# The early rows gathered into the root products' tile, and the pool of row buffers opened inside the branch

## The chip, the cores and the metric

The kernel runs on one core of one Trainium2 chip. The metric is the device time of one execution in microseconds; where several executions are compared, their median is used.

## What is computed

A graph of 6250 nodes with 256 features each and 100000 edges, sorted by their destination. Three layers of message passing, then a layer norm over the sum with the input. Cut to what matters:

```python
ew = edge_attr @ edge_w + edge_b                      # 100000 x 256, from 32 attributes
rel_masks = [(edge_type == i) for i in range(3)]
inv_cnt = [1.0 / max(segment_sum(m, dst), 1.0) for m in rel_masks]
for l in range(3):
    residual = x
    msg = relu(x[src] * ew)
    out = 0
    for i in range(3):
        h = segment_sum(msg * rel_masks[i][:, None], dst) * inv_cnt[i][:, None]
        out = out + h @ weights[l, i]
    out = out + x @ roots[l] + biases[l]
    x = residual + relu(out)
return layernorm(x_in + x)
```

## The kernel before

**Units of work.** The edges are cut into tiles of 128; two tiles are a *pair* (391 pairs), and two pairs share one buffer of gathered rows, a tile named `xs` of 128 x 2 x 2 x 256 floats, 4 KB in each partition. Nodes are cut into 49 tiles of 128. `schedule` (L879) writes out by hand in which order the pairs are taken (`order`: pairs 64 to 390, then 63 down to 0; below, "pair n" is the n-th in this order) and at which step each node tile is finished (`starts`).

**Ahead of the branch.** `tile_gnn_resnorm_kernel` (L934) loads the indices, brings them into the layout of the tiles (`src_i`, `seg`, `place_i`), and tests whether the edges are sorted closely enough (`flag`). The branch at L1072 then runs `ordered_path`; `general_path` is for other inputs and doesn't run here. While the test is still under way, the rows of the first six pairs (`FIRST`, L873) are gathered already (L1017 to L1021): `room` (L921) asks the pool `rows` for a buffer, `gather_pair` (L926) issues two indirect DMAs from GpSimd's queue, one for each tile of 128 edges. Six pairs make twelve gathers and three buffers. The pool has `ROWS` = 8 buffers and is opened at L966, ahead of the branch.

**Inside the branch** one loop per layer (L784) walks over the pairs, one pair a step, and issues for several pairs at once, each at its own distance ahead:

- 9 pairs ahead (`AHEAD`, L463), `gather` (L589): for a layer's first six pairs it takes the buffers that were filled early, else, at every second pair, a new buffer by `room`, and the two gathers of L928. GpSimd has hardly any other work, so its queue holds these gathers one after the other; a gather into a buffer waits for the last reader of the buffer's earlier content.
- 7 and 6 pairs ahead, in layer 0 alone: the edge attributes are transposed on TensorE (L607) and kept by ScalarE (L615), and written to DRAM for the other layers.
- 4 pairs ahead, `make_ew` (L617): TensorE forms the edge weights in PSUM (L623).
- 3 pairs ahead, `weigh` (L641, VectorE, L645) multiplies the gathered rows in place by the edge weights, and `bound` (L647, ScalarE, L649) applies the relu in place.
- 2 pairs ahead, `one_hot` (L651): VectorE makes the matrices of destinations.
- `reduce` (L661): TensorE sums the rows of the pair by destination and relation into PSUM (L665); it is the last reader of the buffer. In layer 0 it also counts the edges (the bf16 products).
- one or two pairs behind (`LAG`), `add` (L670): VectorE adds the sums into the ring `acc` (L683).

**Root products and node tiles.** For each node tile, x @ roots + bias is formed ahead of time (`root_turn`, `root_turned`, `root_mul`, `root_keep`, L685 to L699) and kept in one of the `ROOTS` = 24 places of `x_root` (L487), 1 KB each in a partition. The place is `at_root` (L775). When a node tile's edges are all summed, `node_mul` and `node_end` (L703, L734) multiply by the weights, add to the place in `x_root` (L742), apply the relu and the residual (L745) and write the tile to `x_mid` in DRAM (L747), from where the next layer gathers.

**From layer to layer.** The first six pairs of the next layer are gathered at the end of a layer (`gather_early`, L627), into buffers of the same pool, before node tile 0 is done; what node tile 0 lacks is added afterwards (`complete`, L633). All other gathers of the next layer wait until `x_mid` is written to the end.

The order of the instructions on each engine is as the program issues them; buffers and waits between engines are set by the tile framework.

Of the kernel before, what the change touches and what calls it, by code (L numbers as in the profile page):

```python
# [8 lines left out]
F32 = mybir.dt.float32  # L9
# [430 lines left out]


@with_exitstack
def ordered_path(ctx, tc, x, edge_attr, weights, roots, biases, edge_w, edge_b, out, src, src_i, seg, place_i, consts, rows,
                 first_rows, node_i):


# [4 lines left out]
    P = 128  # L451
    N, D = x.shape
# [20 lines left out]
    ident, ones, iota_w = consts  # L473
# [6 lines left out]
    big = ctx.enter_context(tc.tile_pool(name="big", bufs=1))  # L480
# [3 lines left out]
        nc.scalar.dma_start(ew_sb[row + A:row + A1, :], edge_b[None, :])  # L484

    x_all = big.tile([P, NT, D], F32, name="x_all")
    x_root = big.tile([P, ROOTS, D], F32, name="x_root")  # L487


    acc = big.tile([P, DC + 1, R, ASIDE + 2 * P + WIN], F32, name="acc")  # L490
# [23 lines left out]
    came_i = came.bitcast(I32)  # L514

    edge = ctx.enter_context(tc.tile_pool(name="edge", bufs=2))
    wpool = ctx.enter_context(tc.tile_pool(name="wpool", bufs=1))
    o_pool = ctx.enter_context(tc.tile_pool(name="o_p", bufs=1, space=PSUM))
    r_pool = ctx.enter_context(tc.tile_pool(name="r_p", bufs=1, space=PSUM))
# [53 lines left out]
    def layer(l, r_sb, b_sb, ats, early, pools):  # L573
# [198 lines left out]

        node_at = {s: c for c, s in enumerate(starts)}
        turns_of = [node_at[s] for s in sorted(node_at)]
        at_root = {c: j % ROOTS for j, c in enumerate(turns_of)}  # L775
        root_at = {}

        for j, c in enumerate(turns_of):
# [78 lines left out]
    with tc.manual_schedule():  # L857
        state = (*load_root(0), {}, first_rows)
        for l in range(L):
            with ExitStack() as pools:  # L860
                state = layer(l, *state, pools)
# [8 lines left out]
ROOTS = 24  # L870
GROUP = 8
ROWS = 8
FIRST = 6  # L873
# [5 lines left out]
def schedule(N, E, lag):  # L879

    P = 128
    U = -(-E // (2 * P))
    NT = -(-N // P)
    done = []
    for c in range(NT):
        edges = E * min(1.0, (P * (c + 1) / N) ** 0.5)  # L890
        done.append(U if c == NT - 1 else min(U, -(-int(edges) // (2 * P)) + 4))
    K = -(-done[0] // GROUP) * GROUP
    order = list(range(K, U)) + list(range(K - 1, -1, -1))
    moved = done[1] - K + lag
    starts = [0] * NT
    step = moved
    for c in range(2, NT):
        step = starts[c] = max(done[c] - K + lag + 1, step + 4)

    whole = U - int(0.55 * K)  # L900
    starts[1] = max(whole + lag, step + 4)
    starts[0] = max(U + lag - 1, starts[1] + 4)

    node = lambda e: int(N * min(1.0, max(0.0, e / E)) ** 2)
    least = [node(2 * P * u - ASTRAY) for u in range(U)]
    most = [node(2 * P * u + ASTRAY) for u in range(U)]


    for p, u in enumerate(order, lag):
        if u >= K:  # L910
            assert all(p <= starts[c] or least[u] >= P * (c + 1) for c in range(2, NT))
            assert p <= moved or least[u] >= 2 * P
            assert all(p < starts[c] or least[u] >= P * c for c in range(8, NT, 8))
            for b in range(RING // P + 1, (most[u] + WIN - 1) // P + 1):
                assert (moved + 2 if b - RING // P == 1 else starts[b - RING // P] + 3) < p
        else:
            assert most[u] <= 2 * P and (p <= starts[1] or most[u] + WIN <= P)
    return order, starts, moved, least, most


def room(rows, D):  # L921

    return rows.tile([128, 2, 2, D], F32, name="xs", bufs=ROWS)


def gather_pair(nc, xs, x_rows, src_i, u):  # L926
    for i in range(2):
        nc.gpsimd.indirect_dma_start(  # L928
            out=xs[:, u % 2, i, :], out_offset=None, in_=x_rows[:, :],
            in_offset=bass.IndirectOffsetOnAxis(ap=src_i[:, 2 * u + i:2 * u + i + 1], axis=0))  # L930
# [3 lines left out]
def kernel(ctx, tc, x, src, dst, edge_attr, edge_type, weights, roots, biases, edge_w,  # L934
# [4 lines left out]
    P = 128  # L939
    N, D = x.shape  # L940
# [11 lines left out]
    keep = ctx.enter_context(tc.tile_pool(name="keep", bufs=1))  # L952
    ident = keep.tile([P, P], F32, name="ident_o")
    make_identity(nc, ident)
    ones = keep.tile([1, P], F32, name="ones_o")
    nc.vector.memset(ones, 1.0)
    iota_w = keep.tile([P, WK], F32, name="iota_w")
    nc.gpsimd.iota(iota_w, pattern=[[1, WK]], base=0, channel_multiplier=0,
                   allow_small_or_imprecise_dtypes=True)
    node_i = keep.tile([P, 1], F32, name="node_i")  # L960
    nc.gpsimd.iota(node_i, pattern=[[0, 1]], base=0, channel_multiplier=1, allow_small_or_imprecise_dtypes=True)
    src_i = keep.tile([P, TC], I32, name="src_io")
    seg = keep.tile([P, TC], F32, name="seg_o")
    place_i = keep.tile([1, (U + 1) // 2], I32, name="place_i")
    flag = keep.tile([1, 1], I32, name="flag")
    rows = ctx.enter_context(tc.tile_pool(name="rows", bufs=ROWS))  # L966

    with tc.tile_pool(name="look", bufs=1) as look, tc.tile_pool(name="look_p", bufs=2, space=PSUM) as look_p, \
            tc.manual_schedule():
# [47 lines left out]
        first_rows = {}  # L1017
        for u in schedule(N, E, 1)[0][:FIRST]:
            if u // 2 not in first_rows:
                first_rows[u // 2] = room(rows, D)  # L1020
            gather_pair(nc, first_rows[u // 2], x, src_i, u)  # L1021
        dst_t = by_tile("dst")

# [47 lines left out]
    unordered = nc.values_load(flag[0:1, 0:1], min_val=0, max_val=1)  # L1071
    with tc.If(unordered == 0):  # L1072
        ordered_path(tc, x, edge_attr, weights, roots, biases, edge_w, edge_b, out, src, src_i, seg, place_i,
                     (ident, ones, iota_w), rows, first_rows, node_i)
    with tc.If(unordered > 0):
        general_path(tc, x, src, dst, edge_attr, edge_type, weights, roots, biases, edge_w, edge_b, out)

# [25 lines left out]
```

## Time and profile before

| | us |
|---|---|
| median of 3 runs | 3021.46 (3019.87 to 3021.53) |
| the profiled execution | 3018.21 |
| its span, first to last instruction | 3016.4 |
| mean granted TensorE clock | 0.942 |

| engine | busy us | share of the span |
|---|---|---|
| TensorE, matmuls (PE) | 2789.6 | 92% |
| TensorE, weight loads (PEld) | 2252.3 | 75% |
| VectorE (DVE) | 2080.6 | 69% |
| ScalarE (ACT) | 987.1 | 33% |
| GpSimd (POOL) | 2236.2 | 74% |

The costliest groups of instructions are these; each row has the line, the engine and the operation, what is written and read, the count, and after the bar the busy time, the mean time of one in ns, and the engine's idle time ahead of them.

```profile
L928 POOL DMA_INDIRECT xs<-x_mid,src_io x1564 | 1488.9, 952 | 503.5 <-issue 416.8
...
L665 PE MATMUL h_p<-oh,xs 128*128 128x120 f32 x9384 | 1346.3, 295 | 28.2 <-DVE acc L683 12.5
...
L645 DVE TENSOR_TENSOR xs<-ew_p,xs 128x512 f32<-128x512 f32 x1176 | 753.2, 682 | 558.1 <-DMA xs<-x_mid,src_io 362.0
...
L928 POOL DMA_INDIRECT xs<-in_x_dram,src_io x782 | 745.5, 953 | 255.3 <-issue 198.9
```

Times in the profile are microseconds from the start of the span. In a timeline each row gives the start, the duration, the engine, the line, the operation, what it writes and reads, and in brackets how long the engine sat idle before it and what ended that. "issue" stands for idle time that the profile puts down to nothing. In the views of the waits a row gives the engine, what waited, what for, the total in us, the number of times and the longest. A table by stage gives for each stretch its length, the busy time of PE, PEld, DVE, ACT and POOL with the number of instructions, the granted TensorE clock, the DMA engines' share and the GB/s moved. Layer 0 runs to about 1003 us, layer 1 to about 2003, layer 2 to the end.

### The profile page before, as it was taken

Reading aid. Unit: us, or ns where it says so; the run is one execution under the profiler, and the core shown is the slowest. Engines: PE = TensorE matmul, PEld = TensorE weight load, DVE = VectorE, ACT = ScalarE, POOL = GpSimd, SP = SyncE. Lnnn points to the kernel's source line nnn. Section 1 sums busy time; section 2 is a strip of 40 time slices with the busy share of each in tenths; the row PEclk is TensorE's granted clock in tenths of the full one; section 3 lists DMA queues with packets and bytes.
Section 4 is the critical chain, followed back from the end, with each engine's and each line's share of the span. In section 5 each row is a group of like instructions: output and inputs, shape, how many; then the busy total and the mean of one; then the engine's idle time right before and its main releaser. Section 6 shows DMA issues by size and latency. Waiting matters only on the chain.

```text
span 3016.4 us, 55782 instructions
## 1 busy us (share of the span) xinstructions
PE 2789.6 (92%) x18114; PEld 2252.3 (75%) x18114; DVE 2080.6 (69%) x5865; ACT 987.1 (33%) x1354; POOL 2236.2 (74%) x2355
## 2 busy tenths in 40 slices
PE   6899999999999889999999999889999999999997
PEld 5777878888877667777777777667777777777775
DVE  6676767777776556666666667556667777877765
ACT  4444444444444222222222222212222222322221
POOL 6777777777777677777777777767777777777775
PEclk9999999999999899999999999878999999999888
DMA  5655555555555444444444445434554444444443
GB/s 154 176 162 161 166 165 151 149 158 156 159 156 145 144 125 137 139 132 140 134 142 144 144 137 149 151 116 140 151 149 146 147 147 149 142 144 144 135 139 97
DMA packets 274682, 438.87 MB, mean 145 GB/s; under 512 B 145004, under 2 KB 180032, under 8 KB 274384
## 3 DMA queue, kind: packets, MB, share of 16 engines
q0 software_dynamic: 112608, 307.65, 35.1%
q1 hardware_dynamic: 154720, 119.64, 13.4%
q10 hardware_dynamic: 7056, 7.92, 0.9%
q8 instruction: 149, 2.44, 0.3%
q14 instruction: 149, 1.22, 0.1%
HBM read 389.94 MB, written 45.09 MB: 144 GB/s over the span
## 4 chain that ended last, share of the span: by engine, by line
PE 56%; DMA 16%; POOL 10%; issue 8%; DVE 7%; ACT 2%; DVEq 0%; ACTq 0%; POOLq 0%; SPq 0%
PE h_p L665 25%; PE ew_p L623 16%; DMA xs<-x_mid,src_io 12%; POOL xs L928 10%; PE o_p L711 9%; DVE xs L645 4%; DMA xs<-in_x_dram,src_io 4%; PE r_p L696 3%; PE turn_p L607 1%; ACT xs L649 1%; DVE x_root L742 1%; DVE acc L683 1%; PE r_p L688 1%; PE o_p L637 0%; PE o_p L715 0%
## 5 line engine op out<-in xcount | busy, mean ns | idle before, releaser
L928 POOL DMA_INDIRECT xs<-x_mid,src_io x1564 | 1488.9, 952 | 503.5 <-issue 416.8
L665 PEld LDWEIGHTS h_p<-oh,xs 128*128 128x128 f32 x9384 | 1214.2, 204 | 245.9 <-issue 190.0
L665 PE MATMUL h_p<-oh,xs 128*128 128x120 f32 x9384 | 1346.3, 295 | 28.2 <-DVE acc L683 12.5
L649 ACT ACTIVATE xs<-xs 128x1024 f32<-128x1024 f32 x588 | 620.2, 1055 | 1857.3 <-DVE xs L645 1792.3
L645 DVE TENSOR_TENSOR xs<-ew_p,xs 128x512 f32<-128x512 f32 x1176 | 753.2, 682 | 558.1 <-DMA xs<-x_mid,src_io 362.0
L623 PE MATMUL ew_p<-ew_sb,at 33*128 33x256 f32 x4692 | 861.0, 418 | 151.3 <-DVE xs L645 149.2
L928 POOL DMA_INDIRECT xs<-in_x_dram,src_io x782 | 745.5, 953 | 255.3 <-issue 198.9
L623 PEld LDWEIGHTS ew_p<-ew_sb,at 33*128 33x128 f32 x4692 | 502.5, 191 | 393.8 <-DVE xs L645 192.1
L683 DVE TENSOR_TENSOR acc<-h_p,acc 128x240 f32 (+1 forms) x1173 | 517.7, 441 | 209.7 <-PE h_p L665 125.3
L655 DVE TENSOR_SCALAR oh<-iota_w,seg_o 128x120 f32<-128x120 f32 x2346 | 512.9, 293 | 0.0
L711 PE MATMUL o_p<-w_sb,acc 128*128 128x256 f32 (+1 forms) x1716 | 442.4, 395 | 4.9 <-DVE acc L683 4.9
L711 PEld LDWEIGHTS o_p<-w_sb,acc 128*128 128x128 f32 (+1 forms) x1716 | 319.1, 198 | 41.7 <-DVE acc L683 6.3
L742 DVE SCALAR_TENSOR_TENSOR x_root<-o_p,inv,x_root 128x256 f32<-128x256 f32 (+1 forms) x429 | 205.7, 480 | 47.0 <-PE o_p L711 39.4
L696 PE MATMUL r_p<-r_sb,t_s 128*128 128x256 f32 x588 | 160.7, 397 | 0.1
L659 ACT ACTIVATE oh_b<-oh 128x480 bf16<-128x480 f32 x196 | 117.9, 602 | 101.3 <-DVE oh L655 99.6
L728 ACT ACTIVATE acc<-zero_o 128x768 f32<-128x768 f32 (+1 forms) x150 | 140.5, 937 | 29.1 <-PE r_p L711 19.1
L696 PEld LDWEIGHTS r_p<-r_sb,t_s 128*128 128x128 f32 x588 | 106.6, 202 | 9.2 <-ACT t_s L692 0.3
L665 PE MATMUL h_p<-oh_b,full_ones 128*128 128x120 bf16 x782 | 107.5, 220 | 0.0
L607 PE MATMUL turn_p<-ident_o,an 128*128 128x128 f32 x391 | 79.4, 286 | 10.7 <-DMA an<-in_edge_attr_dram 6.1
L665 PEld LDWEIGHTS <-full_ones 128*128 128x128 bf16 x782 | 81.9, 105 | 2.5
L699 DVE TENSOR_TENSOR x_root<-r_p,b_sb 128x256 f32<-128x256 f32 x147 | 61.1, 416 | 24.0 <-PE r_p L696 19.5
L615 ACT ACTIVATE at<-turn_p 128x256 f32<-128x256 f32 x196 | 71.7, 366 | 2.7 <-PE turn_p L607 2.7
(93 smaller groups left out, 526.6 us busy)
## 6 DMA issues: line engine op xcount, KB each, us to landing
at<-at_all SPq DMA_DIRECT2D x96, 512.0 KB
xs<-x_mid,src_io POOLq DMA_INDIRECT x1564
at_all<-at SPq DMA_DIRECT2D x48, 512.0 KB
xs<-in_x_dram,src_io POOLq DMA_INDIRECT x782
an<-in_edge_attr_dram SPq DMA_DIRECT2D x97, 128.0 KB
x_mid<-x_all SPq DMA_DIRECT2D x96, 128.0 KB
x_all<-in_x_dram ACTq DMA_DIRECT2D x8, 768.0 KB
x<-in_x_dram SPq DMA_DIRECT2D x48, 128.0 KB
```

The lines of the kernel that those rows point to most:

```text
L623: nc.tensor.matmul(ew_ps[q][i][:, k, :], ats[2 * q // GROUP][i * UP:i * UP + A1, (2 * q + k) % GROUP, :], ew_sb[i * UP:i * UP + A1, :], st ...
L645: nc.vector.tensor_mul(there, ew_ps[q][i][:, :n, :], there)
L649: nc.scalar.activation(there, there, AF.Relu)
L655: nc.vector.tensor_scalar(ohs[q][:, t, :], iota_w, seg[:, 4 * q + t:4 * q + t + 1], None, op0=ALU.is_equal)
L659: nc.scalar.activation(oh_bs[q][:, :n], ohs[q][:, :n], AF.Copy)
L665: nc.tensor.matmul(h_ps[u][:, d, :], xs[u // 2][:, u % 2, i, d * P:(d + 1) * P] if d < DC else full_ones, (ohs if d < DC else oh_bs)[u // ...
L683: nc.vector.tensor_tensor(there, h_ps[u][:, :CH].rearrange("p c (r w) -> p c r w", r=R), there, op=ALU.add)
L696: nc.tensor.matmul(rs[c][:, 1, :], t_ss[c][:, d, :], r_sb[:, d, :], start=(d == 0), stop=(d == DC - 1))
L711: nc.tensor.matmul(o_p[:n, j, :], acc[:, d, r, slot:slot + n], w_sb[:, r * DC + d, :], start=(d == 0), stop=(d == DC - 1))
L728: nc.scalar.activation(acc[:, :CH, :, slot:slot + P], zero[:, :, None, None].to_broadcast([P, CH, R, P]), AF.Copy)
L742: nc.vector.scalar_tensor_tensor(root, o_p[:n, j, :], inv[:n, c, r:r + 1], root, op0=ALU.mult, op1=ALU.add)
L928: nc.gpsimd.indirect_dma_start(out=xs[:, u % 2, i, :], out_offset=None, in_=x_rows[:, :], in_offset=bass.IndirectOffsetOnAxis(ap=src_i[:, ...
```

## The change

The rows gathered ahead of the branch no longer take buffers of the pool `rows`. They go into `x_root`, whose 24 places are free at that time: four places make up one buffer for two pairs, three buffers take places 0 to 11. `x_root` is therefore made ahead of the branch and handed to `ordered_path`. The places of the root products are shifted by 12, so that the first twelve root products go to places 12 to 23 and the thirteenth is the first to go to a place that held early rows. The pool `rows`, with eight buffers as before, is opened inside `ordered_path`.

```diff
-def ordered_path(ctx, tc, x, edge_attr, weights, roots, biases, edge_w, edge_b, out, src, src_i, seg, place_i, consts, rows,
+def ordered_path(ctx, tc, x, edge_attr, weights, roots, biases, edge_w, edge_b, out, src, src_i, seg, place_i, consts, x_root,
                  first_rows, node_i):
...
     x_all = big.tile([P, NT, D], F32, name="x_all")
-    x_root = big.tile([P, ROOTS, D], F32, name="x_root")
...
     edge = ctx.enter_context(tc.tile_pool(name="edge", bufs=2))
+    rows = ctx.enter_context(tc.tile_pool(name="rows", bufs=ROWS))
...
-        at_root = {c: j % ROOTS for j, c in enumerate(turns_of)}
+        at_root = {c: (j + 2 * FIRST) % ROOTS for j, c in enumerate(turns_of)}
...
     flag = keep.tile([1, 1], I32, name="flag")
-    rows = ctx.enter_context(tc.tile_pool(name="rows", bufs=ROWS))
+
+    x_root = keep.tile([P, ROOTS, D], F32, name="x_root")
...
         for u in schedule(N, E, 1)[0][:FIRST]:
             if u // 2 not in first_rows:
-                first_rows[u // 2] = room(rows, D)
+                j = 4 * len(first_rows)
+                first_rows[u // 2] = x_root[:, j:j + 4, :].rearrange("p (k i) d -> p k i d", k=2)
             gather_pair(nc, first_rows[u // 2], x, src_i, u)
...
-                     (ident, ones, iota_w), rows, first_rows, node_i)
+                     (ident, ones, iota_w), x_root, first_rows, node_i)
```

## The prediction, made before the changed kernel was run

> **What bounds the kernel now.** I read the engine totals first, then the gathers' own line, then the waits, then the timelines of GpSimd (POOL) and TensorE (PE). The totals seem to say that PE is the bound:
>
> ```profile
> PE 2789.6 (92%) x18114; PEld 2252.3 (75%) x18114; DVE 2080.6 (69%) x5865; ACT 987.1 (33%) x1354; POOL 2236.2 (74%) x2355
> ```
>
> They mislead. The page counts a gather (L928) as its 0.95 us; between two gathers POOL has another 0.30 us of issue. The POOL timeline shows both: starts stand 1.25 us apart whenever nothing stops it, so 2346 gathers take 2346 x 1.25 = 2933 us of the 3016.4 us span. The waits agree: VectorE's multiply (L645) sat idle for landing gathers 203 times in layers 1 and 2, 74 times in layer 0, its longest waits:
>
> ```profile
> DVE xs L645 <- DMA xs<-x_mid,src_io: 362.0, 203, 4.9
> DVE xs L645 <- DMA xs<-in_x_dram,src_io: 97.6, 74, 5.7
> ```
>
> From 150 us on, the multiply of most buffers starts 1.9 to 3 us after the end of its last gather: the arithmetic follows POOL's heel. So POOL's rate sets the end, and only POOL's stops can be won back. I went through all 2346 gathers for gaps over 0.45 us; these are the large ones (start, duration, idle before):
>
> ```profile
> 57.41 0.95 POOL L928 DMA_INDIRECT xs<-in_x_dram,src_io  x1 [6.42 <-issue]
> ...
> 94.84 1.60 POOL L928 DMA_INDIRECT xs<-in_x_dram,src_io  x1 [2.64 <-issue]
> ```
> ```profile
> 1023.17 0.94 POOL L928 DMA_INDIRECT xs<-x_mid,src_io  x1 [5.00 <-DMA x_mid<-x_all]
> ...
> 1038.50 0.95 POOL L928 DMA_INDIRECT xs<-x_mid,src_io  x1 [5.61 <-issue]
> ...
> 1045.92 1.00 POOL L928 DMA_INDIRECT xs<-x_mid,src_io  x1 [2.71 <-issue]
> ```
> ```profile
> 2017.28 0.94 POOL L928 DMA_INDIRECT xs<-x_mid,src_io  x1 [4.31 <-DMA x_mid<-x_all]
> ...
> 2029.28 0.94 POOL L928 DMA_INDIRECT xs<-x_mid,src_io  x1 [2.27 <-issue]
> ...
> 2041.19 0.94 POOL L928 DMA_INDIRECT xs<-x_mid,src_io  x1 [7.21 <-issue]
> ```
>
> The remaining ones are 0.53 at 391.93 and 1.44, 0.55 and 0.50 at 2844.82, 2850.08 and 2854.02. The view names no releaser ("issue"), so I asked which reader had just ended. The gather at 57.41 is the 33rd, the first of the ninth buffer (pairs 16 and 17). PE's timeline there, pairs 6 and 7:
>
> ```profile
> 54.45 1.15 PE L665 MATMUL h_p<-oh,xs 128*128 128x120 f32 x8
> 55.43 0.27 PE L665 MATMUL h_p<-oh_b,full_ones 128*128 128x120 bf16 x2
> 55.54 1.11 PE L665 MATMUL h_p<-oh,xs 128*128 128x120 f32 x8
> 56.48 0.27 PE L665 MATMUL h_p<-oh_b,full_ones 128*128 128x120 bf16 x2
> ```
>
> Were eight buffers in turn, the ninth would take the first's place, whose last reader (pair 1) ended at 45.1; the gather would have started at 51.3. It started 0.7 us after pair 7, the reader of the fourth buffer. So only five buffers turn, 4 to 8: the three that hold the first six pairs, taken ahead of the branch, do not come back inside it. Layer 1 says the same: its sixth buffer (pairs 10, 11) started at 1038.50, 0.7 us after the sums of pairs 0 and 1:
>
> ```profile
> 1033.99 3.77 PE L665 MATMUL h_p<-oh,xs 128*128 128x120 f32 x16
> ```
>
> **The change, part by part.** *Eight buffers in turn instead of five.* The pool now lies inside the branch and the first rows elsewhere, so a gather waits for the buffer eight back. In layer 0 the first to wait is pair 22's, the 45th gather; POOL reaches it at 10.93 + 44 x 1.25 = 66, its buffer came free at 56.8. The 61st, which stops at 94.84 now, would wait for pair 15, summed by 73.0, and POOL is there at 86. In layer 1 pair 16 is first: 1023.17 + 20 x 1.25 = 1048.2, against a release at 1037.8. In layer 2 the same sum gives 2042.3, where the first buffer came free before 2029.28; for the next it is 2047.3 against 2041.19. None waits. What goes, less the 0.30 us of issue that stays:
> - layer 0: 6.12 + 2.34 + 0.23 = 8.7 us
> - layer 1: 5.31 + 2.41 = 7.7 us
> - layer 2: 1.97 + 6.91 + 1.14 + 0.25 + 0.20 = 10.5 us
>
> Together 26.9 us. The 5.00 and 4.31 us for x_mid stay: no buffer feeds them, the last node tile of the layer does.
>
> Who is late next? The arithmetic, which did not itself get faster and must catch up with a POOL that is further ahead. In layers 1 and 2 it can: between 1045 and 1900 PE is busy 797 of 855 us, between 2045 and 2900 794 of 855, and it waited for VectorE's multiply, hence for gathers. 58 and 61 us of room hold 7.7 and 10.5. The last 1.6 us of layer 2 arise at 2850; 2900 to the end still has 21 us of PE room, some of it after the last gather (2995.5). I take both in full. The stages, with PE's busy time first after the length:
>
> ```profile
> 100.00:500.00 400.00, 388.23 (x2861) 320.86 (x2860) 288.33 (x778) 182.36 (x296) 302.56 (x320) 0.98 0.58 162
> 500.00:850.00 350.00, 346.73 (x2559) 286.92 (x2558) 269.49 (x733) 165.71 (x249) 265.27 (x279) 1.00 0.55 156
> 850.00:1003.00 153.00, 143.49 (x992) 118.14 (x991) 103.04 (x278) 64.04 (x98) 116.12 (x122) 0.89 0.54 150
> ...
> 1045.00:1900.00 855.00, 797.06 (x4969) 638.60 (x4967) 564.30 (x1617) 232.43 (x275) 646.93 (x680) 0.95 0.46 139
> ...
> 2045.00:2900.00 855.00, 794.14 (x4943) 636.70 (x4943) 630.84 (x1851) 243.77 (x321) 646.83 (x679) 0.95 0.49 147
> ```
>
> Layer 0 also has the transposes and the count matmuls, and there it is tight: 100 to 850 us PE is busy 735.0 of 750, 850 to 1003 143.5 of 153. That leaves 24.5 us of room for 8.7. Bounds: nothing (PE is full and what POOL wins only fills buffers) and 8.7. The nearer row is VectorE's 97.6 us of waiting for gathers in this layer, 11.7 of them after 900 us, at its very end; I take 7.4, most of it.
>
> *First rows in x_root.* The same twelve gathers of the same 4 KB per partition into another place, and POOL's order is unchanged. The new orderings: a root product must wait for the early rows' sums (L699 on VectorE; behind it queue the additions into acc and the multiplies, which PE's next sums wait for). With the shift by 12, root products 0 to 11 go to places 12 to 23; number 12, the first onto an early place, comes at step 51 of the schedule, near 160 us, and the early rows are summed by 52.4. Cost 0, covered by some 100 us; if the cover were gone it would stall VectorE for at most one sum, 1.3 us. No trace shows gathers into x_root. Upper bound: each waits for the one before to land, 11 x 1.9 = 21 us at the start; lower bound 0, no reason for a gain. The nearest row, four gathers into one buffer at a 1.25 us step, says 0, and I take 0. The shift itself renames places for VectorE alone: 0. The pool's buffers lie elsewhere in memory: POOL's first gather into one, at 26.13, could meet tiles of the stage ahead of the branch, whose last reader (L1068) ended at 23.7: 0.
>
> *A rule against it.* The Trainium skill (Perfetto Trace Analysis, Identifying the Most-Contended Engine) calls the engine of highest occupancy the one to work on, and for TensorE puts the weight loads' share in place of the matmuls'. Here that is 75% against POOL's 74%: by the rule PE comes first, and stops of POOL would be worth nothing, 3021. The row says otherwise, 1.25 us per gather fills 97% of the span, since issue time is not in the 74%. I go by the row.
>
> **The sum.** 7.4 + 7.7 + 10.5 = 25.6 us. The profiled execution took 3018.21 us (span 3016.4), so 2992.6 for it; it lay 3.25 us under the median of 3021.46. Against that median: 2995.9.
>
> **Rivals.**
> 1. *PE takes layer 0.* For: 98% busy from 100 to 850 us. Against: VectorE's waits for gathers up to the layer's end. Layers 1 and 2 alone give 18.2 us: 3003.3. Chance 0.12.
> 2. *No change.* The five-buffer reading is wrong, or the first rows' new place leaves the turn at five, or the longer lead comes back as a longer wait for x_mid. Against: two layers fit five and not eight. 3021.5. Chance 0.06.
> 3. *Slower: the granted clock in layer 0.* The granted clock falls to a half in short stretches: 17 us of 100 to 850 (mean 0.98 and 1.00 in the rows above), but 79 us of 1045 to 1900 (0.95). Price: each microsecond at half clock stretches PE's work by 0.5 us. It decides once layer 0 loses its 24.5 us of room, the 18.2 us of the other layers and 6 more: 49 us, 97 us more of half clock in this one layer. At 100 us: 3028.8. For: PE would have less room. Against: half clock stands at the layers' ends, where PE waits, and the change takes waits away. Chance 0.05.
>
> The forecast itself: 0.76, with 2989 (all 26.9 us off the profiled execution, less some scatter) to 3001. 0.01 stays unnamed, on the slow side.
>
> **How the numbers follow.** Faster is cases forecast and 1: 0.88. A run of this kernel can tell about 0.2%, 6 us, from no change. Same is 0.06, slower 0.06. The range runs from 2989 to 3007: the likeliest case and the most of rival 1.
>
> **What would show it.** On POOL no gap at the 33rd and 61st gather nor at pairs 10 and 12 of layers 1 and 2; the x_mid waits still 4 to 5 us; the layers' last gathers earlier by about 7, 15 and 26 us. In layer 0, a multiply that starts late behind its gather until well past 300 us and is back at 2 us at the end. I am wrong if POOL still stops at these gathers, if x_mid's wait grows by what was won, or if the multiplies of late layer 0 lag.

## The result and the profile after

| | kernel before | changed kernel |
|---|---|---|
| median of 6 runs, us | 3020.66 (3015.11 to 3024.66) | 2995.57 (2991.06 to 3000.81) |
| ratio, 95% interval | 1 | 0.9917 (0.9904 to 0.9931) |
| profiled execution, us | 3018.21 | 2991.06 |
| its span, us | 3016.4 | 2989.3 |
| start of the last gather of layer 0, 1, 2, us | 1002.2, 1997.0, 2994.5 | 992.2, 1978.4, 2966.7 |

The change took 25.1 us from the median (20.8 to 29.0 by the interval) and 27.1 us from the span of the profiled executions. The profiled execution of the changed kernel is the fastest of its six, so part of the 27.1 is scatter. The totals of the changed kernel, from its page:

```profile
PE 2763.4 (92%) x18114; PEld 2239.0 (75%) x18114; DVE 2084.1 (70%) x5865; ACT 986.4 (33%) x1354; POOL 2236.1 (75%) x2355
```

POOL's busy time is the same to 0.1 us: the gathers took as long as before, POOL only stopped less. Of the twelve gaps over 0.45 us between two gathers, two are left, the waits for x_mid at the changes of layer. The first fence is the POOL timeline around the 33rd gather, which now starts at 51.23, the next two those around the stops that are left:

```profile
49.98 0.95 POOL L928 DMA_INDIRECT xs<-in_x_dram,src_io  x1 [0.30 <-issue]
51.23 0.95 POOL L928 DMA_INDIRECT xs<-in_x_dram,src_io  x1 [0.30 <-issue]
52.48 0.95 POOL L928 DMA_INDIRECT xs<-in_x_dram,src_io  x1 [0.30 <-issue]
```
```profile
1007.24 0.95 POOL L928 DMA_INDIRECT xs<-x_mid,src_io  x1 [0.30 <-issue]
1012.61 0.94 POOL L928 DMA_INDIRECT xs<-x_mid,src_io  x1 [4.43 <-DMA x_mid<-x_all]
1013.86 0.95 POOL L928 DMA_INDIRECT xs<-x_mid,src_io  x1 [0.30 <-issue]
```
```profile
1993.55 0.94 POOL L928 DMA_INDIRECT xs<-x_mid,src_io  x1 [0.30 <-issue]
1998.81 0.94 POOL L928 DMA_INDIRECT xs<-x_mid,src_io  x1 [4.32 <-DMA x_mid<-x_all]
```

VectorE still waits for landing gathers, as long as before in layers 1 and 2 (364.0 us, 362.0 before), a little less in layer 0 (83.0, 97.6 before):

```profile
DVE xs L645 <- DMA xs<-x_mid,src_io: 364.0, 199, 4.9
...
DVE xs L645 <- DMA xs<-in_x_dram,src_io: 83.0, 80, 5.6
```

### The profile page after: what moved, and what is told of

It reads as the page before. It is cut to its first block, busy times and chain, and to the rows that moved or that the text cites. A ratio compares the mean times of both kernels' runs of the same rounds, so it can differ in the third digit from the quotient of the medians.

```text
span 2989.3 us, 55660 instructions
## 1 busy us (share of the span) xinstructions
PE 2763.4 (92%) x18114; PEld 2239.0 (75%) x18114; DVE 2084.1 (70%) x5865; ACT 986.4 (33%) x1354; POOL 2236.1 (75%) x2355
## 3 DMA queue, kind: packets, MB, share of 16 engines
q1 hardware_dynamic: 154720, 119.64, 13.6%
## 5 line engine op out<-in xcount | busy, mean ns | idle before, releaser
L649 ACT ACTIVATE xs<-xs 128x1024 f32<-128x1024 f32 (+1 forms) x585 | 617.1, 1055 | 1819.1 <-DVE xs L645 1752.8
L645 DVE TENSOR_TENSOR xs<-ew_p,xs 128x512 f32<-128x512 f32 x1170 | 749.3, 682 | 518.2 <-DMA xs<-x_mid,src_io 364.0
L623 PE MATMUL ew_p<-ew_sb,at 33*128 33x256 f32 x4692 | 846.1, 417 | 153.8 <-DVE xs L645 152.8
L928 POOL DMA_INDIRECT xs<-in_x_dram,src_io x770 | 732.8, 952 | 234.6 <-issue 190.7
L623 PEld LDWEIGHTS ew_p<-ew_sb,at 33*128 33x128 f32 x4692 | 496.2, 191 | 387.4 <-DVE xs L645 188.8
L711 PE MATMUL o_p<-w_sb,acc 128*128 128x256 f32 (+1 forms) x1716 | 434.5, 390 | 4.8 <-DVE acc L683 4.8
L728 ACT ACTIVATE acc<-zero_o 128x768 f32<-128x768 f32 (+1 forms) x150 | 140.4, 936 | 32.6 <-PE r_p L711 17.8
```

Source lines behind the costliest of these rows:

```text
L623: nc.tensor.matmul(ew_ps[q][i][:, k, :], ats[2 * q // GROUP][i * UP:i * UP + A1, (2 * q + k) % GROUP, :], ew_sb[i * UP:i * UP + A1, :], st ...
L645: nc.vector.tensor_mul(there, ew_ps[q][i][:, :n, :], there)
L649: nc.scalar.activation(there, there, AF.Relu)
L711: nc.tensor.matmul(o_p[:n, j, :], acc[:, d, r, slot:slot + n], w_sb[:, r * DC + d, :], start=(d == 0), stop=(d == DC - 1))
L728: nc.scalar.activation(acc[:, :CH, :, slot:slot + P], zero[:, :, None, None].to_broadcast([P, CH, R, P]), AF.Copy)
L928: nc.gpsimd.indirect_dma_start(out=xs[:, u % 2, i, :], out_offset=None, in_=x_rows[:, :], in_offset=bass.IndirectOffsetOnAxis(ap=src_i[:, ...
```

## The experiments

Two questions were open: whether the number of buffers in turn is the whole cause or the place of the first rows and of the pool has a part in it, and whether POOL or TensorE sets the end of layer 0. My theory: five buffers turned, because the three of the first rows never came back, and every microsecond that POOL stops is a microsecond of the whole. The main rival: the place, or TensorE. All times are against the kernel before on the same chip; "us saved" is one minus the ratio, times that kernel's median (3014 to 3021). The changed kernel itself stands at 25.1. The intervals reach 3 to 8 us to either side, so differences of a few us between two rows are read from the traces, not from this table. One more run, e11_pe_all, stands in the text below, since the kernel before took 3769 us on its chip.

| run | what differs from the changed kernel | ratio, 95% interval | us saved |
|---|---|---|---|
| e2_turn5 | 5 buffers | 1.0001 (0.9988 to 1.0013) | -0.3 |
| e3_turn6 | 6 buffers | 0.9955 (0.9938 to 0.9972) | 13.6 |
| e4_turn7 | 7 buffers | 0.9920 (0.9895 to 0.9946) | 24.1 |
| e5_ahead8 | pool of 8 opened ahead of the branch, no second branch | 0.9900 (0.9875 to 0.9926) | 30.1 |
| e6_pool_late | POOL busy elsewhere for 25 us in layer 0 | 0.9994 (0.9983 to 1.0005) | 1.8 |
| e7_pe_12us | a sixth of layer 0's transposes twice | 0.9920 (0.9902 to 0.9938) | 24.2 |
| e7_pe_36us | half of them twice | 0.9927 (0.9909 to 0.9945) | 22.1 |
| e12_pe_all | all of them twice | 0.9912 (0.9886 to 0.9937) | 26.5 |
| e8_first8 | 8 pairs early, 22 root places | 0.9923 (0.9905 to 0.9942) | 23.3 |
| e9_first4 | 4 pairs early | 0.9934 (0.9917 to 0.9950) | 19.9 |
| e10_two_ahead | (kernel before, 2 pairs ahead of the branch) | 0.9941 (0.9924 to 0.9958) | 17.8 |

### How many buffers turn

Three runs change one number of the changed kernel.

```diff
-ROWS = 8
+ROWS = 5
```

> The changed kernel with a pool of 5 buffers instead of 8: first rows still in x_root, pool still inside the branch. If the number of buffers in turn is the whole cause, this is the kernel before again: within 5 us of it, POOL stopping at the 33rd and 61st gather and at pairs 10 and 12 of layers 1 and 2. If the place of the first rows, the shift of the root products or the place of the pool brought part of the gain, that part stays: up to 25 us under the kernel before.

It is the kernel before again. POOL stops at the 33rd and 61st gather and behind x_mid at pairs 10 and 12 of layers 1 and 2, as before; it stops at the 65th too (2.70 us) and no longer near 2850 us. The timeline at the 33rd gather of this run, to be held against the 57.41 of before:

```profile
49.76 0.94 POOL L928 DMA_INDIRECT xs<-in_x_dram,src_io  x1 [0.30 <-issue]
60.29 0.95 POOL L928 DMA_INDIRECT xs<-in_x_dram,src_io  x1 [9.60 <-issue]
```

The first rows' new place, the shift of the root products and the pool's new place are all in this run, and together they bring nothing that shows (-0.3 us, within 4).

With `ROWS = 6`:

> The changed kernel with 6 buffers. In the trace of the changed kernel I held each gather's start against the end of the sums of the buffer six back: the gathers would come too early by at most 5.6 us in layer 0, 3.8 in layer 1, 1.2 in layer 2. If stops of POOL count one to one, this is about 10 us over the changed kernel, some 15 under the kernel before. If a longer lead brings something of its own (smoother arrivals, a better clock), 6 buffers lose more than that.

13.6 us saved where 15 were expected, with the interval from 8.4 to 18.7. Its stops are 2.03, 1.26 and 0.72 in layer 0, none in layer 1, and 2.47, 7.22 and 0.66 in layer 2; the first is at the 37th gather, one buffer later than with five:

```profile
57.59 0.94 POOL L928 DMA_INDIRECT xs<-in_x_dram,src_io  x1 [2.03 <-issue]
```

The sum was nearly right, its layers were not: layer 1 lost nothing, layer 2 about 9 us. I had held the gathers against the release times of one execution of the changed kernel, and these move from run to run: the first multiply of layer 2 starts 15.2 us after that layer's first gather in the changed kernel and 20.6 us after it here, the latest of all runs at this speed.

With `ROWS = 7`:

> The changed kernel with 7 buffers. By the same sum only one gather would be early, by 0.6 us in layer 0. If stops of POOL are the whole cause, this equals the changed kernel within 3 us, 25 under the kernel before, and the eighth buffer is not needed. If the depth itself counts, it lies between 6 and 8 buffers.

24.1 us saved, and no stop but the two for x_mid. The last gathers of the layers start within 1 us of those with eight buffers (992.1, 1978.6, 2965.8). Seven are enough; the eighth buffer buys nothing here.

### The place of the pool

```diff
+    rows = ctx.enter_context(tc.tile_pool(name="rows", bufs=ROWS))
     x_root = keep.tile([P, ROOTS, D], F32, name="x_root")
...
-    rows = ctx.enter_context(tc.tile_pool(name="rows", bufs=ROWS))
     wpool = ctx.enter_context(tc.tile_pool(name="wpool", bufs=1))
...
-    with tc.If(unordered > 0):
-        general_path(tc, x, src, dst, edge_attr, edge_type, weights, roots, biases, edge_w, edge_b, out)
```

> The changed kernel with the pool of 8 buffers opened ahead of the branch, where it was before, and the first rows in x_root as in the change. The second branch, for other inputs, is left out to make room (it does not run). If it is the three buffers held by the first rows that count, all eight turn here too: 25 us under the kernel before. If opening the pool inside the branch is what counts, five turn or the time stays at the kernel before, 3021.

All eight turn, and POOL has the two stops for x_mid and no other. The pool may stay ahead of the branch; what counts is that no buffer of it is given out there. The 5 us beyond the changed kernel lie behind the work: the last gathers start at 993.6, 1979.5 and 2967.1, near those of the changed kernel (992.2, 1978.4, 2966.7), and the last store of the output leaves at the same time in both, first the changed kernel, then this run:

```profile
2981.48 0.34 SPq L764 DMA_DIRECT2D out_dram<-x_all  x1
```
```profile
2981.45 0.34 SPq L763 DMA_DIRECT2D out_dram<-x_all  x1
```

From there to the end of the span it takes 2.9 us here and 7.8 in the changed kernel. I put that down to the branch left out; no run leaves out the branch alone, so this is not shown.

The same from the other side, on the kernel before:

```diff
-        for u in schedule(N, E, 1)[0][:FIRST]:
+        for u in schedule(N, E, 1)[0][:2]:
...
-            if p < FIRST:
+            if p < (2 if l == 0 else FIRST):
```

> The kernel before, its pool ahead of the branch and its first rows in it, but only the first two pairs gathered ahead of the branch: one buffer held instead of three. Theory: seven turn, the stops go as in the run with seven; but POOL is idle from its fourth gather (15.9 us) until the branch is taken (about 23.9 us), and what POOL loses there it does not get back: 25 less 8, some 17 us under the kernel before. If the three held buffers are not the cause, the kernel before plus up to 8 us.

17.8 us saved (12.7 to 22.9) where 17 were expected. The stops at the old places are gone in all three layers with one buffer held instead of three: three gaps over 0.45 us are left, the two for x_mid and this one, ahead of the fifth gather. POOL's row and VectorE's first row inside the branch:

```profile
20.54 1.09 POOL L928 DMA_INDIRECT xs<-in_x_dram,src_io  x1 [4.74 <-DVE ring_i L1061]
```
```profile
23.65 0.06 DVE L493 MEMSET zero_o<- 128x1 f32 x1
```

POOL stopped before the branch for 4.7 us, not 8, since it is inside the branch 3 us earlier than VectorE. So the mechanism stands, and by the sum some 20 us would have been due; the interval holds both.

### Who sets layer 0

POOL first: 60 small instructions in its queue.

```diff
+            if l == 0 and it == 100:
+                idle = edge.tile([P, D], F32, name="x0", bufs=2)
+                for _ in range(60):
+                    nc.gpsimd.iota(idle, pattern=[[1, D]], base=0, channel_multiplier=0,
+                                   allow_small_or_imprecise_dtypes=True)
             if pair(AHEAD) is not None:
                 gather(pair(AHEAD))
```

> The changed kernel with 60 small instructions added to POOL's queue in layer 0, ahead of the gathers of pair 109: some 20 us in which POOL gathers nothing. If POOL's pace sets the end of layer 0, the end moves by the whole length of that stretch, read from the trace, about 20 us over the changed kernel. If TensorE sets layer 0, the buffers filled ahead (up to eight) and its own room hide most of it.

The POOL timeline at that place:

```profile
283.16 0.95 POOL L933 DMA_INDIRECT xs<-in_x_dram,src_io  x1 [0.30 <-issue]
284.11 24.81 POOL L790 IOTA x<- 128x256 f32 x60
309.08 0.96 POOL L933 DMA_INDIRECT xs<-in_x_dram,src_io  x1 [0.15 <-issue]
```

Two gathers that should start 1.25 us apart start 25.9 apart: 24.7 us lost. The last gather of layer 0 comes 23.2 us after that of the changed kernel, and 25.1 us saved become 1.8, which is 23.3 us. Nothing of the stop is hidden: the last gathers of layers 1 and 2 come 24.1 and 25.5 us later.

Then TensorE, with transposes made twice (`% 6`, `% 2` and, for e12_pe_all, `% 1`):

```diff
-            for k in pairs_of(q):
+            for k in (*pairs_of(q), *(pairs_of(q) if q % 6 == 0 else ())):
                 nc.tensor.transpose(turns[q][:, k, :], ans[groups.index(q // 2) % 3][:, q % 2 * 2 + k].rearrange("p i a -> p (i a)"),
                                     ident)
```

> The changed kernel with every sixth buffer's transposes of layer 0 made twice: about 33 x 0.37 = 12 us more work on TensorE. If POOL sets layer 0 and TensorE has the 20 to 25 us of room that the table by stage shows, the time stays within 3 us of the changed kernel. If TensorE is the bound of layer 0, it grows by 12.

> The same with every second buffer: about 98 x 0.37 = 36 us more on TensorE in layer 0. By the room of 20 to 25 us read from the table, 11 to 16 us over the changed kernel; if TensorE is the bound throughout layer 0, 36; if the busy figure counts waiting as work and the true room is larger, under 5.

The first load cost nothing that shows (24.2 us saved), the second 3.0 us against the changed kernel, which is inside the interval. But I had mis-sized the second load: 0.37 us is what the profile shows for a row of two transposes that overlap. Start to start one transpose takes 0.109 us, so the 196 added ones are 21 us, and the 66 of the first run 7. 21 us still lie under the 24.5 us of room that the table by stage gives, so this could not tell the two readings of the room apart. Hence one more:

> The changed kernel with the transposes of layer 0 made twice for every buffer. The run with every second buffer showed that one added transpose costs TensorE 0.109 us from start to start, so this adds 391 x 0.109 = 43 us to layer 0. Two readings of TensorE's room there: the table by stage leaves 24.5 us, which makes 18 us over the changed kernel; VectorE's waits for gathers (80 us in the changed kernel, 40 left with 21 us added) leave about as much again, which makes less than 5.

That run is inconclusive: on that chip the kernel before took 3769 us and this one 3794 (ratio 1.0066, 1.0027 to 1.0105). In its trace POOL stops 360 times between gathers, the engines sit idle for long times that the profile puts down to nothing or to something outside the core, and the mean granted clock is 0.85. Why is open. The same kernel on another chip:

> The same kernel once more, since in the run before this one the kernel before itself took 3769 us, a quarter more than in all others, and that run can't be held against them. As there: 43 us more work for TensorE in layer 0; 18 us over the changed kernel by the room in the table by stage, less than 5 by VectorE's waits for gathers.

26.5 us saved (19.0 to 34.4): 43 us more work on TensorE in layer 0 cost nothing that can be measured. The last gather of layer 0 starts at 992.8, as in the changed kernel (992.2). This is where the added work went; VectorE's waits between 100 and 990 us in the changed kernel and in this one:

```profile
DVE xs L645 <- DMA xs<-in_x_dram,src_io: 79.9, 79, 5.6
```
```profile
DVE xs L645 <- DMA xs<-in_x_dram,src_io: 23.2, 18, 3.2
```

57 us of waiting went, and layer 0 ends when it did. The room was nearly used up: VectorE's multiply runs 4 to 9 us behind its gather from 500 to 890 us, and is level with the changed kernel again by 912. TensorE's busy time from 100 to 850 us, first number after the length, rose by only 9 us from 738.8 in the changed kernel, while some 33 of the 43 us were added there:

```profile
100.00:500.00 400.00, 398.36 (x3095) 335.78 (x3094) 295.42 (x796) 186.91 (x302) 302.85 (x319) 1.00 0.57 164
500.00:850.00 350.00, 349.58 (x2668) 294.28 (x2667) 267.42 (x724) 165.91 (x246) 265.22 (x279) 1.00 0.54 154
```

So the table had counted stretches as busy in which TensorE could still take work. The edge weights' matmuls show most of it, first in the changed kernel and then here, from 100 to 850 us; busy time stands behind the bar, and the counts differ by 1%:

```profile
L623 PE MATMUL ew_p<-ew_sb,at 33*128 33x256 f32 x1220 | 190.4, 404 | 10.9 <-DVE xs L645 10.6
```
```profile
L623 PE MATMUL ew_p<-ew_sb,at 33*128 33x256 f32 x1204 | 173.5, 402 | 2.1 <-DVE xs L645 2.1
```

Another part came from the granted clock, which was higher in this run: from 100 to 1000 us the changed kernel spent 41 us at half clock and this one 14, which is worth some 14 us of work at the full clock. So not all of the 43 us went into room that was there before. Whether the added work raised the clock or the clock differed by chance, one trace of each doesn't show.

### The two stops that are left

They wait for x_mid, 4.3 to 4.6 us at each change of layer in nearly every run (5.2 once in e7_pe_36us, for no reason that I found). More gathers in that time seemed free.

```diff
-ROOTS = 24
+ROOTS = 22
...
-FIRST = 6
+FIRST = 8
```

> The changed kernel with 8 pairs gathered early instead of 6, in all layers, and 22 places for the root products instead of 24 to make room. The two stops that POOL has left, 4.4 and 4.3 us, wait for x_mid; four more gathers, 5.0 us, fit into that time. If POOL's stops count one to one, about 8 us less than the changed kernel, 33 under the kernel before. If the two pairs more that must be completed by hand at the start of a layer lie on the path, or the root products come too late, nothing or a loss of up to 10.

Nothing gained: 23.3 us saved, and the stops are 4.57 and 4.48. VectorE's row and SyncE's row at the end of layer 0 show why:

```profile
1010.79 0.49 DVE L745 SCALAR_TENSOR_TENSOR x_all<-x_root,x_all 128x256 f32<-128x256 f32 x1
```
```profile
1017.64 0.32 SPq L747 DMA_DIRECT2D x_mid<-x_all  x1
```

The node tile is ready at 1011.3, its store leaves at 1017.6, 2.1 us after the last early gather ended (1015.5). The early gathers read x_mid, and the store into it waits, as I read it, until they have landed. In the changed kernel the store leaves at 1010.1, 1.9 us after the node tile is ready and 2.0 us after the last early gather. So I tried fewer, `FIRST = 4`:

> The changed kernel with 4 pairs gathered early instead of 6, in all layers. In the run with 8 pairs the last store into x_mid of a layer left only when the early gathers had landed, 6.4 us after VectorE had its rows ready (in the changed kernel 1.9 us after). If that store waits for the early gathers, which read x_mid, then with 4 pairs it leaves as soon as VectorE is done, the stop behind the early gathers grows from 4.4 to about 7 us, and each of the two layer changes loses some 3 us: about 6 over the changed kernel, 19 under the kernel before. If the store waits for something else (SyncE's queue, the loads), it keeps its delay and each layer change loses the whole 5 us of the four gathers: 10 over the changed kernel.

At the end of layer 0 the store leaves 0.03 us after VectorE, and POOL then stops for 9.4 us; at the end of layer 1 it leaves 0.4 us after VectorE, 2.0 us after the last early gather, and the stop stays at 4.5. 19.9 us saved, 5.2 less than the changed kernel; 19 were expected. In the two traces with 8 and 4 early pairs the 2346 gathers also took 2239 us in sum, against 2232 to 2235 in all others. That is 4 us or more, as much as these two runs are about, and its cause is open, so their times are weaker evidence than the rows. In every trace the next gather starts 2.45 to 2.48 us after the store. The last store and gather of layer 0 with four pairs:

```profile
1011.66 0.32 SPq L747 DMA_DIRECT2D x_mid<-x_all  x1
```
```profile
1014.15 0.94 POOL L928 DMA_INDIRECT xs<-x_mid,src_io  x1 [9.37 <-DMA x_mid<-x_all]
```

So a stop of 4.4 us is a landing of about 1.9 us and a store of about 2.5 us, unless the node tile is later still. Neither more nor fewer early gathers shortened the two changes of layer together. The wait can't simply be left out: an early gather that met the new rows of node tile 0 would have them added a second time in `complete`. It was not tried.

## Why the prediction was right

**Five of eight.** Right, shown from three sides: five buffers in the changed kernel give the kernel before, eight ahead of the branch give the changed kernel, and one held buffer instead of three removes the stops in the kernel before.

**POOL's stops count one to one.** Right: 26.9 us of stops were named and all of them went, and a stop of 24.7 us put in on purpose came back as 23.3. That the span fell by 27.1, so near to 26.9, is partly luck: the median fell by 25.1, give or take 4.

**The layers.** By the starts of the last gathers, 10.0 us were won in layer 0, 8.6 from there to the end of layer 1 (18.6 in all) and 9.1 in layer 2. Predicted were 7.4, 7.7 and 10.5. In layer 0 I took 7.4 of 8.7 because TensorE looked tight; that discount was wrong. The stops themselves went in full in all three layers, 8.7, 7.7 and 10.5; the rest is scatter. In layer 0 the gathers happened to take 1.2 us less in sum, in layer 2 1.4 us more, and the wait for x_mid behind layer 0 shrank from 5.00 to 4.43. So layer 2's term was not too large. The prediction of 2995.9 and the measured 2995.6 agree more closely than either is known: the median stands to about 4 us, and without the wrong discount the sum would have been 26.9 instead of 25.6. That part of the nearness is luck.

**The waits for x_mid.** They stayed at 4 to 5 us, as foretold, but not for the reason given, that the last node tile feeds them. Ahead of layer 2 the store left 5.2 us after that tile was ready in the kernel before and 5.4 in the changed one, and 1.9 and 1.8 us after the last early gather. It follows the early gathers, and these follow POOL, so what POOL won didn't come back as a longer wait. The tile and its store in the kernel before, where the last early gather ended at 2012.96:

```profile
2009.19 0.42 DVE L745 SCALAR_TENSOR_TENSOR x_all<-x_root,x_all 128x256 f32<-128x256 f32 x1
```
```profile
2014.83 0.32 SPq L747 DMA_DIRECT2D x_mid<-x_all  x1
```

Ahead of layer 1 the node tile did come last before the change (the store left 0.03 us after it); in the changed kernel the early gathers do.

**The room of TensorE in layer 0.** The size was off. The table gave 24.5 us, and 43 us more work fitted in. Rival 1, TensorE takes layer 0, falls with it: layer 0 gave its whole 8.7. VectorE's multiply did follow late behind its gather for longer, as foretold, 10 us at 137 us, but was back at 3 us by 200, sooner than the "well past 300" of the prediction; later it rose again to 8 us near 385, as in the kernel before (394).

**The first rows in x_root.** Cost 0, as taken: the twelve gathers start in the same 1.25 us step.

**The rule of the Trainium skill** (Perfetto Trace Analysis, Identifying the Most-Contended Engine), read by the weight loads' busy share, put TensorE with 75% ahead of POOL's 74%, and would have made the change worth nothing. It would have been 25 us off; the row of 1.25 us per gather decided. The same page's Optimization Strategy comes near to what was found: "Consistent bubbles", the same gap repeating on the engine that should be saturated, "can mean there isn't enough SBUF/PSUM for the next tile to be allocated". Here the gaps were single ones, ten in 3016 us, and too few buffers in turn were behind them all the same.

**The slower rival,** a lower granted clock in layer 0, did not come: the granted clock was 0.98 and 1.00 in the two stages from 100 to 850 us, as before.

## What to carry to other kernels

An engine that only issues transfers can be the bound at 74% busy: count its instructions times the step from start to start, and look at every stop. When a stop has no named releaser, find which reader ended just before it; the distance in buffers tells how many really turn. A buffer given out ahead of a branch and read inside it may not come back, as the three here did not. Room on an engine is better read from how long its consumers wait for somebody else than from its busy share, and a probe that adds work settles it.

## What the runs showed of the hardware that was not expected

An indirect gather of 128 rows of 1 KB keeps POOL busy for 0.95 us, and the next starts 0.30 us later, in all runs and with little scatter (the medians are 0.946 to 0.949 us; fewer than 1 in 100 took over 1.1, the longest 2.09). One transpose more costs TensorE 0.109 us, where the row of two lasts 0.37 to 0.39 us. And one chip ran the kernel before and one experiment a quarter slower (3769 and 3794 us), with idle times that nothing in the profile's view of this core releases. In the experiment there the gathers took as long as elsewhere (2232 us in sum), yet POOL stopped 360 times even with eight buffers, mostly at the first gather of a buffer; the runs on that chip say nothing about this change.
